# Moving three images' expert step from layer 0's front to a place beside layer 1's first convolution, in rounds of four 32-row parts

## The chip, the core and the metric

The kernel runs on one core of one Trainium2 chip. The metric is the device time of one execution in microseconds (us). The core has five engines with queues of their own: PE (matmul, with its weight loads shown apart as PEld), DVE (vector work), ACT (activations), POOL (GpSimd) and SP, which here only issues DMAs. The engines meet through semaphores. SBUF and PSUM are the memories on the core, HBM the one outside.

## The reference

Two residual layers on an fp32 tensor x of 4 images, 64 channels, 256 x 256 pixels. Layer 0 is x + L0(gn(x)), layer 1 the same with L1; gn is a group norm over 32 groups of two channels, whole image.

```python
# L0
h = gelu(conv3x3(x))                        # 64 -> 64
xa, k = split(conv1x1(h))                   # 64 -> 64 + 64
xs = gelu(vertical3(horizontal3(xa)))       # depthwise
gate = top2(softmax(mean_pixels(xs) @ gate_w.T))   # 3 experts per image
out = xs
for i in range(3):                          # ranks of 2, 4 and 8: 14 in all
    out = out + conv1x1(conv1x1(k, w2) * conv1x1(xs, w1), w3) * gate[:, i]
return conv1x1(out, proj)
# L1: weights rounded to 255 steps
h = relu(batchnorm(conv3x3(x)))
h = batchnorm(conv3x3(h))
return relu(h + x)
```

The batch norms run over all four images, so layer 1's second convolution starts only when the first is done for all images. The gate of an image needs the mean of xs over all its pixels.

## The kernel before, in words

An image is held as 128 partitions (64 channels times two row parities or two slots) by 128 pairs of rows. The units are: a group of 2 pairs (512 numbers per partition), an octet of 4 pairs, a chunk of 8 pairs (2048 numbers per partition, 1 MB). An image has 64 groups, 32 octets and 16 chunks.

The kernel has these stages. **Front** of layer 0, image by image: one step handles one octet, with the first convolution (`ps_c`, as a transform with products from the ring `v_ring` that POOL makes at line 413), the depthwise taps (`ps_a`), the projection of xs (`ps_p`), which is added into the chunk of x and written to HBM as `t1_d` (traffic group `t_d<-x`, line 587), and the experts' 14 ranks: `front_k` and `front_q` put k times xs, padded to 16 rows for each of 8 row groups, into the SBUF tile `low` (line 597), 512 numbers per partition for each of the 16 chunks. **Experts' step** ("out"): when an image's front has ended and its gate is known, `gate` scales the third expert matrices by the gate into `wm`, and `out_groups` makes y, the output of layer 0: a matmul of `low` with `wm` into `ps_o` (line 661), DVE adds it to the chunk of `t1_d` that `out_load` fetched (line 663), takes statistics for layer 1's group norm (line 666), and SP writes the chunk to `y_d` in four DMAs (line 671). `out_end` combines the statistics with two small matmuls (`ps_m`, `ps_v`). **First convolution** of layer 1 (`conv1`): for each chunk `conv1_load` fetches `y_d`, ACT applies the group norm (line 695) and makes the upper half of the fp32 split (line 700), DVE makes the lower half, y minus upper (`conv1_lower`, line 707), and PE runs 12 matmuls of 128 x 128 by 512 for each group (line 281); ACT moves the result out of PSUM (line 723), DVE takes statistics (line 728) and ACT's queue writes it to `h1_d`. **Second convolution**, and an **end stage** that adds and writes the output.

One step of `out_groups` works on two 64-row halves of `low` at once: half i of the partitions holds one octet, `wm` has 128 columns for one of two slots, and the two matmuls write two PSUM banks. It yields 1024 numbers per partition, half a chunk, so an image takes 32 such rounds.

The order of the work around the change is written out by hand. `at(step, order, call, ...)` enters a call in a plan; the plan is run through in the order of (step, order), and PE, SP, DVE and POOL take their instructions in exactly that order, each engine waiting only for its own data. ACT's order is the scheduler's. Front steps of image b are 32 b to 32 b + 31, and `CONV1` = 128 is the first step of the first convolution, whose steps are one group each: image b has the 65 steps from 128 + 65 b. The last front steps of image 3 are spread over the first ten of them (`tail`). Image b's out rounds stand in the front steps of image b + 1, one per step from 32 (b + 1) + 4; those of image 3 stand beside the first convolution, one in four steps from step 140:

```python
plan_out(b, CONV1 + 12 if last_one else (b + 1) * F_STEPS + 4, 0.25 if last_one else 1, 2)
```

PSUM is one pool of tiles of two banks: two tiles for "c", one for "a", one for "p"; "p" is shared by `ps_k`, `ps_q`, `ps_p`, `ps_o` and small matmuls. The first convolution uses only one bank of a tile: two tiles up to step 139, then three in turn. Chunks from HBM for the front and for the first convolution come into four buffers of the tag "in"; `out_load` has three buffers ("o"); the halves of a chunk have two buffers, so a chunk's halves can be written when PE has left the chunk two before it.

Of the kernel before, what the change touches and what calls it, by code (L numbers as in the profile page):

```python
# [12 lines left out]
ALU = mybir.AluOpType  # L13
# [5 lines left out]
P = 128  # L19

# [37 lines left out]
def conv_preact_kernel(ctx: ExitStack, tc: tile.TileContext, io, col128, colset, col64):  # L58
# [8 lines left out]
    psum = ctx.enter_context(tc.tile_pool(name="psum", bufs=1, space=PSUM))  # L67
# [4 lines left out]
    def bank(tag, name):  # L72

        return psum.tile([P, 2, GP, W], F32, tag=tag, name=name, bufs=BANKS[tag])

    def small(name):

        return bank("p", name)[:, 0, 0, :]
# [3 lines left out]
    t1_d = [dram.tile([P, NPAIR, W], F32, name=f"t1_d{b}") for b in range(B)]  # L82
    y_d = [dram.tile([P, NPAIR, W], F32, name=f"y_d{b}") for b in range(B)]
# [487 lines left out]
    def front_proj(b, n):  # L571

        ps = bank("p", f"ps_p_{b}_{n}")
        proj = c128("proj")

        rounds(
            *(
                [((ps[:, i], i ^ s, i, proj, xss[b, n][:, s].rearrange("p (a b) -> p a b", b=W), (0, GP)), dict(start=True, stop=True))]
                for i in range(2)
                for s in range(2)  # L580
            )
        )
        k, i = n // 2, 4 * (n % 2)
        t1 = xs_of[b, k][:, i : i + 4, 1 : 1 + W].rearrange("p (q s) w -> p s q w", s=2)
        nc.vector.tensor_tensor(t1, ps, t1, ALU.add)  # L585
        if n % 2 == 1:
            nc.sync.dma_start(t1_d[b][:, k * CPAIR : (k + 1) * CPAIR, :], xs_of[b, k][:, :, 1 : 1 + W])

    def front_q(b, j):
# [7 lines left out]
        nc.vector.scalar_tensor_tensor(low[:, j, :], ps, c128("e_b1"), k_sb.pop((b, j)), ALU.add, ALU.mult)  # L597


    wm, out_bias, ys, st_y = {}, {}, {}, {}  # L600

    def gate(b):
# [26 lines left out]
        for e, (i, j) in enumerate(((3, 4), (0, 5), (1, 2))):  # L629
# [4 lines left out]
        pick = stat.tile([P, 5, 3], F32, tag="pick", name=f"pick_{b}")  # L634
        of = c128("of").rearrange("p (i e) -> p i e", e=3)
        nc.vector.tensor_tensor(pick[:, 0:4, :], keep.unsqueeze(1).to_broadcast([P, 4, 3]), of, ALU.mult)
        nc.vector.tensor_tensor(pick[:, 4, :], keep, pb3, ALU.mult)
        row = stat.tile([P, 5], F32, tag="row", name=f"row_{b}")
        nc.vector.tensor_reduce(row, pick, AX.X, ALU.add)
        wm[b] = lstat.tile([P, 4, C], F32, tag="wm", name=f"wm_{b}")  # L640
        nc.vector.tensor_tensor(
            wm[b], row[:, 0:4].unsqueeze(2).to_broadcast([P, 4, C]), pw3.unsqueeze(1).to_broadcast([P, 4, C]), ALU.mult
        )
        out_bias[b] = stat.tile([P, 1], F32, tag="ob", name=f"ob_{b}")
        nc.vector.tensor_tensor(out_bias[b], row[:, 4:5], c128("proj_b"), ALU.add)
# [5 lines left out]
    def out_groups(b, j):  # L651


        if j == 0:
            st_y[b] = stat.tile([P, NG, 6], F32, tag="st_y", name=f"st_y{b}")
        k, slot = j // 2, j % 2
        ps = bank("p", f"ps_o_{b}_{j}")
        for i in range(2):
            rows = slice(i * C, i * C + C)
            w = wm[b][rows, 2 * slot : 2 * slot + 2, :]  # L660
            nc.tensor.matmul(flat(ps[:, i]), flat(w), low[rows, k, :], start=True, stop=True)  # L661
        y = ys[b, k].rearrange("p (i q s) w -> p s i q w", i=2, s=2)[:, slot]
        nc.vector.scalar_tensor_tensor(y, ps, out_bias[b], y, ALU.add, ALU.add)  # L663
        for i in range(2):
            g = 2 * j + i
            nc.vector.bn_stats(st_y[b][:, g, :], y[:, i])
            if g % CG == CG - 1:
                y = ys.pop((b, k))
                for half in range(2):
                    for slot in range(2):  # L670
                        nc.sync.dma_start(
                            y_v[b][half, slot ^ half][:, k * CG : (k + 1) * CG],
                            y[half * C : half * C + C, slot : CPAIR - 1 + slot : 2],
                        )
# [27 lines left out]
    def conv1_lower(b, k):  # L702
# [4 lines left out]
        nc.vector.tensor_tensor(lower, at_y, upper.bitcast(F32), ALU.subtract)  # L707

    def conv1(b, s):
# [5 lines left out]

        tag = "c" if b == 0 and s < 12 else "cca"[s % 3]
        ps = bank(tag, f"ps_h_{b}_{s}")[:, 0]
# [97 lines left out]
    def plan_out(b, t, per, order):  # L815

        for k in range(NCH):
            at(max(t + int((k - 1.5) * 2 / per) - 1, t - 2), 5, out_load, b, k)
        for j in range(NG // 2):
            at(t + int(j / per), order, out_groups, b, j)  # L820
        e = t + int(NG / 2 / per) + 1
        at_each(((e, 5.5), (e + 1, 5.5), (e + 1, 9.95), (e + 2, 5.5)), out_end(b))
# [10 lines left out]
    def plan_conv1(b):  # L833
        t = CONV1 + b * (NG + 1)
        if b == 0:
            at(t - 3, 0, lambda: halves.append(half_pads([half_tile(first_pool, f"half_10{j}", 2) for j in range(2)])))
            at(t, 12, conv1_open)
        for k in range(NCH):
# [11 lines left out]
    for b in range(B):  # L850
# [3 lines left out]
        last_one = b == B - 1  # L854
        plan_out(b, CONV1 + 12 if last_one else (b + 1) * F_STEPS + 4, 0.25 if last_one else 1, 2)
# [59 lines left out]
    for i, (b, k) in enumerate(chunks):  # L915
# [3 lines left out]
        for n in range(CG):  # L919
# [4 lines left out]
            ps = bank("cacp"[n], f"ps_h2_{b}_{k}_{n}")[:, 0]  # L924
# [63 lines left out]
def _layout(a):  # L988
# [44 lines left out]
    of = np.zeros((4, 2, 2, 2, 16, 3), f)  # L1033
    for i, (group, half) in enumerate(((0, 0), (1, 0), (1, 1), (0, 1))):
        of[i, :, group, half, np.arange(NLOW), expert] = 1.0
# [10 lines left out]
        "of": of.transpose(1, 2, 3, 4, 0, 5).reshape(P, 12),  # L1046
# [38 lines left out]
```

## Time and profile before

| what | value |
|---|---|
| median of 3 runs | 3538.37 us (3536.97 to 3542.3) |
| the profiled execution: its own time, its span | 3536.42 us, 3534.3 us |
| PE busy | 2942.4 us, 83% of the span |
| DVE, ACT, POOL busy | 2248.1, 1672.0, 631.2 us |
| share of the chain of waits that PE holds | 75% |
| DMA moved | 796.33 MB, mean 225 GB/s |
| stages, by their first and last matmuls in the timeline | front from 67 us, first convolution 1526 to 2342 us, second 2352 to 3078 us, end stage to 3534 us |
| out rounds: `ps_o` matmuls, additions (line 663), statistics (line 666) | 144.6, 163.7 and 164.7 us busy, 128 rounds |

The page gives busy times per engine, the span in 40 slices of 88 us, DMA traffic, the chain of work that ended last (followed back from the end, so that each piece is what the next waited for), the costliest groups, and DMA issues. An engine's idle time costs nothing where another engine is the bound; what matters is which wait ends last in the stage.

### The profile page before, as it was taken

What the parts mean: (1) busy time and instruction counts of PE and PEld (TensorE: products, weight loads), DVE (VectorE), ACT (ScalarE), POOL (GpSimd) and SP (SyncE); (2) the same over time, 40 slices, a digit from 0 to 9 for tenths busy, and PEclk for the clock granted to TensorE, in tenths of its full rate; (3) what the DMA queues carried; (4) which work ended last, traced back from release to release, by engine and by line L of the source; (5) the groups of instructions that cost most, each with busy time, mean ns of one, the idle gap of its engine ahead of it and who ended that gap; (6) DMA issues with size and microseconds to landing.
All of it is one profiled execution on the core that took longest, in us unless ns stands there. A gap on an engine that the chain in (4) does not pass through costs nothing.

```text
span 3534.3 us, 60792 instructions
## 1 busy us (share of the span) xinstructions
PE 2942.4 (83%) x25840; PEld 1941.7 (55%) x25840; DVE 2248.1 (64%) x2520; ACT 1672.0 (47%) x1706; POOL 631.2 (18%) x1250
## 2 busy tenths in 40 slices
PE   2999999999999999989999999989999999700000
PEld 1555555554555555547777788878888888600000
DVE  7666688878887777665666544444444444566666
ACT  0444434434433434446555566656666666422223
POOL 2444444433443444400000000000000000000000
PEclk9999999999999999999999999999999999955555
DMA  8564578667776666647776655545555553299999
GB/s 281 147 177 133 159 231 253 207 201 236 242 231 180 182 179 185 190 128 287 262 272 233 233 200 195 199 178 192 200 202 199 197 199 107 95 397 411 413 411 389
DMA packets 344031, 796.33 MB, mean 225 GB/s; under 512 B 19088, under 2 KB 281744, under 8 KB 282064
## 3 DMA queue, kind: packets, MB, share of 16 engines
q1 hardware_dynamic: 326912, 673.42, 56.8%
q10 hardware_dynamic: 16848, 119.02, 8.3%
q8 instruction: 203, 3.33, 0.4%
q14 instruction: 68, 0.56, 0.0%
HBM read 472.03 MB, written 320.34 MB: 224 GB/s over the span
## 4 chain that ended last, share of the span: by engine, by line
PE 75%; DMA 9%; DVE 6%; SPq 5%; ACT 3%; issue 1%; POOL 0%; DVEq 0%; ACTq 0%; POOLq 0%
PE ps_h L281 38%; PE ps_c L370 18%; PE ps_a L370 8%; DMA y_end<-y_d 5%; PE ps_o L661 3%; PE ps_k L561 3%; PE ps_p L370 3%; SPq L972 3%; DMA yn<-y_d 2%; SPq L967 2%; PE ps_q L594 1%; DMA xs_in<-in_x 1%; DVE h L964 1%; ACT v L963 1%; DVE st_x L317 1%
## 5 line engine op out<-in xcount | busy, mean ns | idle before, releaser
L281 PE MATMUL ps_h<-half,w_q 128*128 128x512 f32 x6168 | 1459.3, 397 | 14.6 <-DVE half L707 5.7
L281 PEld LDWEIGHTS ps_h<-half,w_q 128*128 128x128 f32 x6168 | 1162.8, 189 | 324.2 <-ACT h L723 15.6
L413 POOL TENSOR_TENSOR v_ring<-x 128x256 f32<-128x256 f32 x1024 | 596.7, 615 | 159.7 <-PE ps_c L370 109.1
L728 DVE BATCH_NORM_STATS2 st_h<-h 128x6 f32<-128x512 f32 x252 | 173.4, 691 | 356.5 <-ACT h L723 356.3
L370 PE MATMUL ps_c<-v_ring,u 64*64 64x256 f32 (+1 forms) x6472 | 389.0, 371 | 10.2 <-POOL v_ring L413 5.5
L370 PE MATMUL ps_c<-v_ring,c1s 64*64 64x256 f32 (+1 forms) x6472 | 386.6, 368 | 0.5 <-DVE ps_c L481 0.5
L370 PEld LDWEIGHTS ps_c<-v_ring,u 64*64 64x64 f32 x6472 | 254.2, 133 | 238.6 <-issue 79.2
L370 PE MATMUL ps_a<-h,av 64*64 64x512 f32 (+1 forms) x3568 | 381.8, 530 | 2.6 <-DVE t L540 2.6
L370 PEld LDWEIGHTS ps_c<-v_ring,c1s 64*64 64x64 f32 x6472 | 262.0, 133 | 134.5 <-issue 39.2
L928 DVE BATCH_NORM_STATS2 st_h<-h 128x6 f32<-128x512 f32 x256 | 174.0, 690 | 239.5 <-ACT h L927 239.5
L479 ACT ACTIVATE m<-ps_c 128x512 f32<-128x512 f32 x128 | 76.6, 598 | 473.5 <-PE ps_c L370 466.5
L723 ACT ACTIVATE h<-ps_h,m,scale_w 128x512 f32<-128x512 f32 x256 | 196.1, 770 | 206.4 <-PE ps_h L281 202.4
L554 ACT ACTIVATE xs<-t 128x1024 f32<-128x1024 f32 x128 | 135.4, 1058 | 322.1 <-DVE t L543 295.6
L927 ACT ACTIVATE h<-ps_h,m,scale_w 128x512 f32<-128x512 f32 x256 | 197.3, 771 | 182.2 <-PE ps_h L281 181.9
L963 ACT ACTIVATE v<-y_end,shift,gn 128x2048 f32<-128x2048 f32 x64 | 133.8, 2092 | 311.1 <-DMA y_end<-y_d 304.3
L295 DVE TENSOR_TENSOR half<-h,half 128x2304 fp32r<-128x2304 f32 (+1 forms) x65 | 163.8, 2521 | 147.6 <-ACT half L293 147.6
L964 DVE SCALAR_TENSOR_TENSOR h<-h,ss,v 128x2048 f32<-128x2048 f32 x64 | 150.2, 2350 | 150.2 <-ACT v L963 149.7
L585 DVE TENSOR_TENSOR x<-ps_p,x 128x1024 f32<-128x1024 f32 x128 | 156.4, 1222 | 131.4 <-PE ps_p L370 99.0
L370 PEld LDWEIGHTS ps_a<-h,av 64*64 64x64 f32 x3568 | 163.7, 133 | 114.4 <-issue 79.7
L537 DVE SCALAR_TENSOR_TENSOR t<-ps_a,m,t 128x1020 f32<-128x1020 f32 x128 | 163.6, 1278 | 83.7 <-ACT t L536 83.7
L487 ACT ACTIVATE h<-ps_c,c1b 128x512 f32<-128x512 f32 x256 | 176.1, 748 | 36.4 <-PE ps_c L370 36.4
L663 DVE SCALAR_TENSOR_TENSOR y<-ps_o,ob,y 128x1024 f32<-128x1024 f32 x128 | 163.7, 1279 | 18.5 <-PE ps_o L661 15.3
(159 smaller groups left out, 2645.2 us busy)
## 6 DMA issues: line engine op xcount, KB each, us to landing
h_d<-h ACTq DMA_DIRECT2D x113, 1024.0 KB, 4.1
h<-h_d SPq DMA_DIRECT2D x64, 1152.0 KB, 5.1
yn<-y_d SPq DMA_DIRECT2D x60, 1152.0 KB, 8.3
xs_in<-in_x SPq DMA_DIRECT2D x64, 1024.0 KB, 7.7
x<-in_x SPq DMA_DIRECT2D x256, 256.0 KB, 4.9
t_d<-x SPq DMA_DIRECT2D x64, 1024.0 KB, 5.3
y<-t_d SPq DMA_DIRECT2D x64, 1024.0 KB, 7.9
y_d<-y SPq DMA_DIRECT2D x256, 256.0 KB, 5.1
```

Source lines behind the costliest of these rows:

```text
L281: nc.tensor.matmul(ps[:, 0:n, :], w[:, kx, m, :], t[:, i + m : i + m + n, kx : kx + W], start=(j == 0), stop=(j == len(terms) - 1),)
L295: nc.vector.tensor_tensor(lower, y[:, a:e, :], upper.bitcast(F32), ALU.subtract)
L370: last[:] = [nc.tensor.matmul(ps[o, at_out[0] : at_out[1], :], w[i], rhs[i], **flags)]
L413: nc.gpsimd.tensor_tensor(v_ring[:, o : o + 2, p, :], *terms[p])
L487: nc.scalar.activation(h.rearrange("p q (c e) -> p e q c", e=2), c[:, t].rearrange("p (e q c) -> p e q c", e=2, q=GP), AF.Gelu, bias=c1_bi ...
L663: nc.vector.scalar_tensor_tensor(y, ps, out_bias[b], y, ALU.add, ALU.add)
L723: nc.scalar.activation(h, ps, AF.Identity, bias=c128("b1"), scale=w_scale["w1"])
L728: nc.vector.bn_stats(st[:, s, :], h)
L927: nc.scalar.activation(o, ps, AF.Identity, bias=c128("b2"), scale=w_scale["w2"])
L928: nc.vector.bn_stats(st[:, k * CG + n, :], o)
L963: nc.scalar.activation(v, y, AF.Identity, bias=shift[:, b : b + 1], scale=gn2[b][:, 1:2])
L964: nc.vector.scalar_tensor_tensor(h, h, ss2[:, 0:1], v, ALU.mult, ALU.add)
```

## The change

- Images 1 to 3 do their out rounds beside the first convolution: image 1 in steps 142 to 182 (during image 0's convolution), image 2 in 191 to 246, image 3 in 256 to 311, 16 rounds each. Image 0 keeps its 32 rounds in image 1's front.
- A round of images 1 to 3 is a whole chunk: four matmuls, each of a 32-row part of the ranks with a 128-column `wm`, into four PSUM banks (`ps_o`, one buffer). `wm` and its selector `of` have two row layouts in place of four slots. DVE works on the four banks one at a time: an addition and a statistics instruction of 512 numbers each. Image 0's rounds have two 32-row parts.
- `front_q` of images 1 to 3 writes each chunk of ranks to HBM (`low_d`), and `low_load` reads it back beside `out_load`, into the two buffers of tag "k".
- `front_proj` writes a chunk of `t1_d` in three DMAs in place of one, with the lower 64 partitions' two slots exchanged.
- `conv1_lower` runs on GpSimd in place of DVE.
- At step 140 the PSUM pool is closed and a new one opened: four one-bank tiles for both convolutions and the small matmuls, and one of four banks for `ps_o`.

```diff
+    def banks_open():
+        banks0.close()
+        psum.append(ctx.enter_context(tc.tile_pool(name="psum1", bufs=1, space=PSUM, reuse_waits="tile")))
...
         if n % 2 == 1:
-            nc.sync.dma_start(t1_d[b][:, k * CPAIR : (k + 1) * CPAIR, :], xs_of[b, k][:, :, 1 : 1 + W])
+            x = xs_of[b, k][:, :, 1 : 1 + W]
+            t1 = t1_d[b][:, k * CPAIR : (k + 1) * CPAIR, :]
+            nc.sync.dma_start(t1[0:C], x[0:C])
+            for slot in range(2):
+                nc.sync.dma_start(t1[C:P, 1 - slot :: 2], x[C:P, slot::2])
...
+        if b > 0:
+            nc.sync.dma_start(low_d[b][:, j, :], low[:, j, :])
...
+    def low_load(b, k):
+        lows[b, k] = work.tile([P, GF], F32, tag="k", name=f"low_{b}_{k}")
+        nc.sync.dma_start(lows[b, k], low_d[b][:, k, :])
+
+    def out_octets(b, k, octets):
...
+        if b == 0:
+            ranks = low[:, k, :]
+            ps = bank("p", f"ps_o_{b}_{k}_{octets[0]}")
+        else:
+            ranks = lows.pop((b, k))
+            ps = psum[1].tile([P, 4, GP, W], F32, tag="o", name=f"ps_o_{b}_{k}", bufs=1)
+        for n, i in enumerate(octets):
+            for g in range(2):
+                rows = slice(64 * i + 32 * g, 64 * i + 32 * g + 32)
+                nc.tensor.matmul(flat(ps[:, 2 * n + g]), flat(wm[b][rows]), ranks[rows], start=True, stop=True)
+        for n, i in enumerate(octets):
+            for g in range(2):
+                y = ys[b, k][:, 4 * i + g : 4 * i + g + 3 : 2, :]
+                nc.vector.scalar_tensor_tensor(y, ps[:, 2 * n + g], out_bias[b], y, ALU.add, ALU.add)
+                nc.vector.bn_stats(st_y[b][:, 4 * k + 2 * i + g, :], y)
+        if 1 in octets:
+            y = ys.pop((b, k))
+            for half in range(2):
+                for g in range(2):
+                    nc.sync.dma_start(
+                        y_v[b][half, g][:, k * CG : (k + 1) * CG],
+                        y[half * C : half * C + C, g::2],
+                    )
...
-        nc.vector.tensor_tensor(lower, at_y, upper.bitcast(F32), ALU.subtract)
+        nc.gpsimd.tensor_tensor(lower, at_y, upper.bitcast(F32), ALU.subtract)
...
-        tag = "c" if b == 0 and s < 12 else "cca"[s % 3]
-        ps = bank(tag, f"ps_h_{b}_{s}")[:, 0]
+        ps = bank("c", f"ps_h_{b}_{s}")[:, 0] if len(psum) == 1 else bank1(f"ps_h_{b}_{s}")
...
+    def plan_out(b, t, e):
+
+        steps = [t + (e - 6 - t) * k // (NCH - 1) for k in range(NCH)]
+        for k in range(NCH):
+            for call in (out_load, low_load):
+                at(steps[k - 2] if k > 1 else t - 1, 0.2, call, b, k)
+            at(steps[k], 2, out_octets, b, k, (0, 1))
+        at_each(((e - 5, 15), (e - 4, 15), (e - 3, 15), (e - 2, 15)), out_end(b))
...
+            at(t + 12, -1, banks_open)
...
-        last_one = b == B - 1
-        plan_out(b, CONV1 + 12 if last_one else (b + 1) * F_STEPS + 4, 0.25 if last_one else 1, 2)
+        if b == 0:
+            plan_out0(F_STEPS + 4)
+        else:
+            step = CONV1 + (b - 1) * (NG + 1)
+            plan_out(b, step + (14 if b == 1 else -2), step + NG - 5)
```

## The prediction, made before the changed kernel was run

> **What bounds the kernel now.** I read the page's slices first, then the chain of waits in the three stages concerned, then the stretches (busy time of each engine in a window), then the groups by shape.
>
> ```profile
> PE   2999999999999999989999999989999999700000
> DVE  7666688878887777665666544444444444566666
> DMA  8564578667776666647776655545555553299999
> ```
>
> PE is at nine tenths from 88 us to 3000 us, in the front and in both convolutions alike. So moving PE work from one stage to the other gains nothing by itself; the change pays only if the step gets cheaper on PE. DMA is the row to watch: it has room in the first convolution now, and most of the step's traffic is being moved there.
>
> The price of a round in the front can be read by comparing two octets without one (image 0, chain of waits) with two that have one (image 3, timeline of PE):
>
> ```profile
> 194.69 3.62 PE ps_c L370 x64
> 204.47 3.62 PE ps_c L370 x64
> 215.24 3.62 PE ps_c L370 x64
> ```
>
> ```profile
> 1260.58 1.96 PE L370 MATMUL ps_c<-v_ring,u 64*64 64x256 f32 x32
> 1262.47 1.13 PE L661 MATMUL ps_o<-low,wm 64*128 64x512 f32 x4
> ...
> 1272.44 1.96 PE L370 MATMUL ps_c<-v_ring,u 64*64 64x256 f32 x32
> ...
> 1283.43 1.94 PE L370 MATMUL ps_c<-v_ring,u 64*64 64x256 f32 x29
> ```
>
> Two steps take 215.24 - 194.69 = 20.55 us without rounds and 1283.43 - 1260.58 = 22.85 us with two, so a round costs 1.15 us: its matmuls, and nothing that hides. Beside the first convolution the chain shows
>
> ```profile
> 1613.75 1.06 PE ps_o L661 x4
> 1614.81 11.41 PE ps_h L281 x48
> 1626.22 1.06 PE ps_o L661 x4
> 1627.28 11.41 PE ps_h L281 x48
> ```
>
> Four groups and a round take 12.47 us. Later, without rounds, the chain has 768 matmuls (64 groups) in 179.87 us: 2.81 a group, 11.24 for four. A round costs 1.23 us there. The clock is at 1.00 in both places.
>
> DMA, by stretches (length; PE, PEld, DVE, ACT, POOL busy; clock; DMA share; GB/s):
>
> ```profile
> 1790.00:1797.00 7.00, 7.00 (x32) 5.64 (x31) 3.88 (x4) 4.35 (x4) 0.00 (x0) 1.00 0.90 197
> 1797.00:1805.00 8.00, 8.00 (x35) 5.68 (x34) 4.15 (x6) 3.16 (x3) 0.00 (x0) 1.00 0.98 401
> 1650.00:1800.00 150.00, 150.00 (x629) 110.81 (x628) 92.39 (x99) 87.18 (x73) 0.56 (x2) 1.00 0.75 263
> ```
>
> With image 3's rounds at a quarter of the later rate, this stage already holds the DMA engines for 0.75 of the time at 263 GB/s, or 263/0.75 = 351 GB/s while they work. With loads of several kinds queued they reach 401; right after y's writes, 197.
>
> **The change part by part**, against the profiled execution (3536.4 us, its span 3534.3), which is 2 us under the median.
>
> *Front.* Images 1 and 2 lose 64 rounds there: 64 x 1.15 = 73.6 us saved. Sixty lie in full steps, four where image 3's last octets mix with the first groups of the convolution. In those four the timeline shows PE waiting 1.46, 0.96 and 1.43 us more on DVE or ACT around `ps_o`, which goes too: another 4 (0 to 8). DVE's part of a round (1.28 + 2 x 0.69) lies beside PE in the front and saves nothing.
>
> *Four parts at once.* 48 rounds of a whole chunk stand where 32 half-chunk rounds of image 3 stood. The trace has no four 32-row parts. Nearest are the four column parts of `ps_k` and `ps_q` (0.96 and 1.08 us for four, from 123.1/128 and 69.1/64) and the two row parts of `ps_o`: a part more costs nothing in either. I take 1.23: 48 x 1.23 - 32 x 1.23 = +19.7. From below 5 less; from above, if only two of the four ran together, 48 x 1.06 = 51 more. The Trainium skill ("TensorE: Matmul & The Clock Gate", Part 3, measured speedup) speaks a little against the change: it states 3.07 times for four 32-row parts, not 4. An estimate by that rule makes a round 1.06 x 4/3.07 = 1.38 us and the sum 15 us dearer; no run here shows it yet.
>
> *DVE.* These groups carry it:
>
> ```profile
> L666 DVE BATCH_NORM_STATS2 st_y<-y 128x6 f32<-128x512 f32 x256 | 164.7, 685 | 4.4
> L707 DVE TENSOR_TENSOR half<-yn,half 128x2304 fp32r<-128x2304 f32 x60 | 152.6, 2543 | 2.6 <-ACT half L700 2.6
> L597 DVE SCALAR_TENSOR_TENSOR low<-ps_q,m,k 128x512 f32<-128x512 f32 x64 | 48.0, 750 | 38.0 <-PE ps_q L594 38.0
> ```
>
> A 512-wide addition out of PSUM takes 0.75 us (line 597 has that shape), so a round is 4 x 0.75 + 4 x 0.69 = 5.8 us of DVE. Image 1's rounds come every 40/15 = 2.67 steps, 2.67 x 2.81 + 1.23 = 8.7 us; with 2.67 statistics of the convolution (1.8) DVE has 7.6 us of work in 8.7. It fits only because the lower halves leave it (2.54 per four steps). For images 2 and 3 a round comes every 3.67 steps, 11.5 us. Cost 0. Queued behind an addition that waits for its chunk are the convolution's statistics, and behind those ACT's next output buffer: if y comes late, that is how it reaches PE. Image 0's rounds cost DVE 0.2 us more, under PE.
>
> *Lower halves on GpSimd.* Line 413's 128x256 subtraction takes 615 ns on POOL, so 2304 columns take 9 x 0.615 = 5.5 us. In steady state a half starts when ACT's copy (2.13) ends, and PE needs it a chunk (11.2 us or more) after that copy could start: over 3 us spare, 0. Where PE waited directly behind it (1598.35 to 1600.97, first chunks) it costs 3 us (0 to 9, as three such halves are on the chain). The rule in "GPSIMD Engine Reference" (4.1, engine selection), which sends two-input elementwise work to VectorE, makes it 4497/2048 x 2304 = 5.1 us as an estimate; the term would be 2.5.
>
> *SP and buffers.* SP gets two more `t_d` issues in all 64 chunks and 48 writes and 48 loads of ranks, 0.3 to 0.6 us each, in queues that wait for data anyway; in the front it loses as many y issues. 0; without that cover, some 1 us a chunk. New waits: `low_load` stands on SP until PE has done the round two before, which y's writes of that round outlast; `ps_o` has one buffer, so PE's next round waits for four additions (about 5.1 us of 8.7). Both 0 while DVE keeps up. One-bank PSUM tiles give the convolution four buffers in place of two or three: 0, at best the 6 us or so of the 15.6 that PE waited for ACT in both convolutions.
>
> *Two more `out_end`* beside the convolution. Image 3's is there already:
>
> ```profile
> 2010.63 0.59 PE L262 MATMUL ps_v_y<-d_y,m 128*128 128x1 f32 x2 [6.38 <-DVE d_y L259]
> ```
>
> It sits behind statistics, which sit behind an ACT that waited 4.76 us for a chunk of y. In the front each cost some 1.5. I take +4 each, 8 - 3 = +5 (-3 to +11).
>
> *Transfers.* Image 1's rounds: ten chunks of the convolution (1.18 in, 1.05 out) and 16 of y (1.05 in, 1.05 out, 0.26 ranks), less 3.7 fetched ahead: 56.4 MB. PE's time there is 40 x 2.81 + 16 x 1.23 = 132 us, so it asks 427 GB/s: more than either rate. At 401 it takes 141 us (+9), at 351 161 (+29). Images 2 and 3: 64.7 MB in 55 x 2.81 + 16 x 1.23 = 174 us, 372 GB/s: 0 at 401, +10 each at 351. A full queue is the nearest row, but SP will leave gaps; I take +17, +4 and +4 = +25 (9 to 49).
>
> Sum: -73.6 - 4 + 19.7 + 3 + 5 + 25 = -24.9 us. From 3536.4 that is 3511.5, and 3513.5 against the median.
>
> **The rivals.** (a) *The transfers hide.* If they run at 401 with what was fetched ahead, and the two `out_end` are free, the sum is -24.9 - 16 - 8 = -49: about 3489. For it: the stretch at 401 with PE at 8.00 of 8. Against: every load of the convolution now stands on SP behind y's writes, which wait for DVE.
>
> (b) *The transfers become the bound, slower than before.* SP issues in order: y's four writes wait for the additions, the next chunk's load waits for an older chunk's writes to land, and convolution loads stand behind both, so the engines idle and then work in the 197 GB/s manner. The three stages move 56.4 + 2 x 64.7 = 185.8 MB in 480 us. The gain is used up when they take 50 us longer, 185.8/530 = 350 GB/s mean: just the rate at which they now work when they work. At 320 they take 580 us, +101 in place of +25, so -24.9 + 76 = +51: 3589.
>
> (c) *Four parts run two by two*: 3513.5 + 51 = 3564. Against it, columns of `ps_k`.
>
> (d) *The front doesn't shorten*, because POOL, SP or the added writes take the rounds' place: 3513.5 + 73.6 = 3587. Image 0's front, at 20.55 us for two steps with the same work, speaks against.
>
> **How the numbers follow.** Forecast 0.50, with its own range 3494 to 3535; (a) 0.19, (b) 0.22, (c) 0.06, (d) 0.03. A measurement can tell about 0.2%, 7 us, from no change. Faster by more: 0.87 of the forecast and all of (a), 0.62. Within: 0.13 of the forecast and a fifth of (b), 0.11. Slower: 0.27. The low end, 3472, takes all good bounds (-24.9 - 16 - 8 - 5 - 4 - 3 - 6 = -67); the high end, 3578, leaves out the far half of (b) and (d).
>
> **What would show it.** Right: two front steps of images 2 and 3 in about 20.6 us; `ps_o` rounds of 1.06 to 1.1 us with eight instructions; over 350 GB/s in image 1's rounds; GpSimd rows of about 5.5 us with no PE wait on them after the first chunks; PE waits of some 20 us in image 1's rounds, released by DMA, ACT or DVE. Wrong: a first convolution that grows by more than the front shrinks, SP rows with long waits at y's writes while DMA is under 0.9; a round of 2 us; or front steps still at 22.8.

## The result, and the profile after

The change makes the kernel slower. Its median is 3618.36 us (3616.68 to 3623.19, four runs) against 3539.14 us before on the same chip: a ratio of 1.0225, 95% interval 1.0208 to 1.0243. The forecast was 3513.5 us and its range ended at 3578. The profiled execution has a span of 3616.6 us, 82.3 above that of before.

The table gives the stages of single profiled executions, in us. A front reaches from the first transform instruction of an image on DVE to that of the next image (image 3's to its own last one); "conv1 0" to "conv1 3" are the first convolution's images, by the ends of ACT's moves out of PSUM, and "between" is the stretch from DVE's last transform instruction of image 3's front to the end of the convolution's step 11, from where "conv1 0" is counted. The second convolution (729 to 731) and the end stage (462 to 465) did not move, with one exception that is named under E17. "Conv1" is the sum of its four images. E1 to E18 are the experiments of the next section.

| kernel | front 0 | 1 | 2 | 3 | between | conv1 0 | 1 | 2 | 3 | conv1 | span |
|---|---|---|---|---|---|---|---|---|---|---|---|
| before | 330.1 | 370.8 | 376.7 | 360.9 | 84.4 | 169.7 | 203.2 | 193.0 | 178.9 | 744.8 | 3534.3 |
| after | 336.3 | 395.6 | 366.5 | 330.8 | 72.8 | 233.7 | 217.8 | 214.9 | 180.7 | 847.1 | 3616.6 |
| E1 statistics' load first | 326.0 | 372.6 | 345.2 | 330.6 | 72.9 | 226.9 | 223.4 | 215.7 | 180.6 | 846.6 | 3562.5 |
| E9 without 50 MB of writes | 329.2 | 371.5 | 345.2 | 332.4 | 71.2 | 201.1 | 206.5 | 205.3 | 178.2 | 791.1 | 3506.1 |
| E10 y in one long write | 329.5 | 372.6 | 343.7 | 331.2 | 72.5 | 218.9 | 206.0 | 204.6 | 181.3 | 810.8 | 3530.0 |
| E11 four long writes | 329.5 | 372.2 | 345.2 | 330.6 | 72.6 | 224.6 | 215.7 | 209.2 | 180.6 | 830.1 | 3549.9 |
| E12 two images, spread | 329.3 | 371.8 | 379.2 | 333.9 | 77.4 | 188.9 | 209.4 | 209.4 | 182.3 | 790.0 | 3548.0 |
| E13 the same, early loads | 329.0 | 371.5 | 378.6 | 334.2 | 77.6 | 181.3 | 198.2 | 197.7 | 180.6 | 757.8 | 3515.6 |
| E14 the change's own steps | 329.5 | 372.6 | 378.9 | 333.8 | 77.5 | 163.9 | 218.5 | 217.3 | 180.1 | 779.8 | 3540.0 |
| E18 long pieces | 329.3 | 372.3 | 381.9 | 333.7 | 74.6 | 171.8 | 202.7 | 192.1 | 179.8 | 746.4 | 3504.4 |

So the loss has two places. The fronts and the stretch behind them gave 9.3 + 11.6 = 20.9 us where 77.6 were forecast. The convolution grew by 102.3 us where 52.7 were forecast. That is 56.7 and 49.6 us beyond the forecast. The two together, 102.3 - 20.9 = 81.4, are the loss.

The slices of the page show where PE lost its nine tenths, and that the DMA row is at eight and nine tenths beside the rounds:

```profile
PE   2999999998999999878899999989999999800000
DMA  8565578766664454379899998545555553299999
```

**The front.** An event from image 1's front. First SP's timeline (start, length, line, traffic): three writes of `t1_d`, the write of the ranks, and only then the loads of the next image's chunk for the statistics.

```profile
547.32 0.89 SPq L601 DMA_DIRECT2D t_d<-x  x1
548.25 2.59 SPq L603 DMA_DIRECT2D t_d<-x  x2
550.94 0.76 SPq L615 DMA_DIRECT2D low_d<-low  x1
551.74 5.74 SPq L322 DMA_DIRECT2D xs_in<-in_x  x2
```

DVE's timeline then shows a statistics instruction before which DVE sat idle for 4.18 us until that load had landed (idle time and its releaser in brackets):

```profile
555.85 1.27 DVE L329 BATCH_NORM_STATS2 st_x<-xs_in 128x6 f32<-128x512 f32 x2
561.30 0.69 DVE L329 BATCH_NORM_STATS2 st_x<-xs_in 128x6 f32<-128x512 f32 x1 [4.18 <-DMA xs_in<-in_x]
```

Behind it on DVE stands the addition of line 597, which empties the bank "p", and for that bank PE waits. The first row is the same work in an undisturbed step:

```profile
536.59 1.92 PE L573 MATMUL ps_k<-h,wk 128*32 128x512 f32 x16
...
563.17 3.64 PE L573 MATMUL ps_k<-h,wk 128*32 128x512 f32 x16 [3.67 <-DVE x L597]
```

The wait costs twice: these matmuls take 3.64 us here and 1.92 in the undisturbed step, and the granted clock is 0.50 from 563 to 567 us. From 480 to 1120 us DVE waited for the statistics' loads 33.5 us in all, 7 times, 5.9 us at the longest:

```profile
DVE st_x L329 <- DMA xs_in<-in_x: 33.5, 7, 5.9
```

In the same window the kernel before has no such wait, and E1, the experiment that issues these loads earlier, has 0.5 us of it.

Where the front is not held up, in image 3's, the chain of waits has the forecast length; two steps take 1312.06 - 1291.56 = 20.5 us:

```profile
1291.56 3.62 PE ps_c L382 x64
...
1302.28 3.62 PE ps_c L382 x64
...
1312.06 3.62 PE ps_c L382 x64
```

**The convolution.** The stretches from the first to the last round of images 1, 2 and 3 (length; PE, PEld, DVE, ACT, POOL busy; clock; DMA share; GB/s):

```profile
1594.00:1767.00 173.00, 140.92 (x589) 98.38 (x588) 107.42 (x160) 69.98 (x58) 46.55 (x10) 0.90 0.89 307
1804.00:1990.00 186.00, 178.67 (x800) 131.96 (x799) 117.89 (x179) 99.90 (x84) 64.97 (x15) 0.99 0.97 343
2022.00:2207.00 185.00, 176.78 (x791) 130.39 (x790) 117.89 (x178) 98.48 (x83) 62.35 (x14) 0.99 0.98 344
```

In the rounds of images 2 and 3 the DMA engines are full (0.97 and 0.98) at 343 and 344 GB/s, with DVE and POOL far from full. In those of image 1 they reach 0.89, and the chain of waits shows a round hand over from transfer to transfer: y's writes (line 697) land, which frees the buffer for the load of y, behind which the ranks are loaded, for which PE waits:

```profile
1671.61 1.55 SPq L697
1673.20 6.23 DMA y_d<-y
1679.57 0.33 SPq L667
1680.00 7.66 DMA low<-low_d
...
1687.79 1.91 PE ps_o L687 x8
```

That reading suggested that an order on SP could mend it. The experiments say otherwise.

### The profile page after: what moved, and what is told of

Same layout as the page of the kernel before. It is cut to its first block, busy times and chain, and to the rows that moved or that the text cites. A ratio compares the mean times of both kernels' runs of the same rounds, so it can differ in the third digit from the quotient of the medians.

```text
span 3616.6 us, 61538 instructions
## 1 busy us (share of the span) xinstructions
PE 2928.0 (81%) x25840; PEld 1956.2 (54%) x25840; DVE 2120.2 (59%) x2584; ACT 1664.6 (46%) x1702; POOL 927.7 (26%) x1314
## 4 chain that ended last, share of the span: by engine, by line
PE 69%; DMA 12%; DVE 7%; SPq 6%; ACT 2%; issue 2%; POOL 1%; ACTq 0%; DVEq 0%; POOLq 0%
PE ps_h L293 34%; PE ps_c L382 17%; PE ps_a L382 8%; DMA y_end<-y_d 5%; PE ps_k L573 3%; PE ps_p L382 3%; SPq L1009 3%; DMA yn<-y_d 2%; DMA xs_in<-in_x 2%; PE ps_o L687 2%; SPq L1004 2%; PE ps_q L610 2%; DMA low<-low_d 1%; DVE st_x L329 1%; DVE h L1001 1%
## 5 line engine op out<-in xcount | busy, mean ns | idle before, releaser
L293 PE MATMUL ps_h<-half,w_q 128*128 128x512 f32 x6168 | 1477.5, 400 | 30.5 <-POOL half L733 16.9
L733 POOL TENSOR_TENSOR half<-yn,half 128x2304 fp32r<-128x2304 f32 (+1 forms) x64 | 297.0, 4640 | 582.8 <-ACT half L726 580.7
L382 PEld LDWEIGHTS ps_c<-v_ring,c1s 64*64 64x64 f32 x6472 | 270.3, 134 | 95.9 <-issue 15.8
L721 ACT ACTIVATE yn<-yn,gn 128x2304 f32<-128x2304 f32 (+1 forms) x64 | 146.9, 2296 | 172.7 <-DMA yn<-y_d 168.7
```

The lines of the kernel that those rows point to most:

```text
L293: nc.tensor.matmul(ps[:, 0:n, :], w[:, kx, m, :], t[:, i + m : i + m + n, kx : kx + W], start=(j == 0), stop=(j == len(terms) - 1),)
L382: last[:] = [nc.tensor.matmul(ps[o, at_out[0] : at_out[1], :], w[i], rhs[i], **flags)]
L733: nc.gpsimd.tensor_tensor(lower, at_y, upper.bitcast(F32), ALU.subtract)
```

## The experiments

Theories: the **order theory** for the front (loads late behind writes on SP); for the convolution the **loop theory** (SP's order makes each round wait for a landing), the **rate theory** (the DMA engines can't carry more), the **GpSimd theory** (the slower halves), and later the **landing theory** (loads issued too late for the time that they take). Each difference in the table of stages is between single executions. Seven kernels with the same convolution traffic (the change, E1 to E3, E5, E6, E8) have a sum of 835.6 to 847.1, and three with that of E13 (E13, E15, E16) one of 757.8 to 769.9. So a difference of up to 12 us between two sums can be chance, and where it matters the medians are given beside it. Of the kernels, E2, E4, E9, E10 and E11 compute other values than the reference.

**E1, the statistics' load first.**

```diff
-at(t + int((k - 1) * CG / per), 11.5, stats_load, b, k, "s", 2)
+at(t + int((k - 1) * CG / per), 5.5, stats_load, b, k, "s", 2)
```

> The changed kernel with one order changed: in the front, the load of the next image's statistics chunk is issued by SP ahead of the step's three t_d writes and the write of ranks, not behind them. Nothing else is moved; the bytes are the same. Order theory (the front lost its gain because the statistics' loads stand on SP and in the queue behind writes that wait for DVE, and DVE in order waits for them): the fronts of images 1 and 2 (395.6 and 366.5 us in the changed kernel) lose 15 to 30 us each, total 3560 to 3590 us; the first convolution stays. Rate theory (the stage asks for more bytes than the DMA engines carry, whatever the order): no stage moves by more than 5 us, total 3612 to 3624. GpSimd theory (the slower lower halves cost the time): no change either, since the fronts have none.

Measured: 3563.22 us, 1.0067 of before (1.0044 to 1.009), 55 us less than the change. Fronts 1 and 2 lost 23.0 and 21.3 us, the convolution stayed at 846.6. The order theory holds for the front: one order on SP was worth nearly all of its missing gain. E2, E3 and E4 ran beside it, without this edit; E5, E6 and E8 to E16 and E18 contain it.

**E2, one write of t1_d.**

```diff
-nc.sync.dma_start(t1[0:C], x[0:C])
-for slot in range(2):
-    nc.sync.dma_start(t1[C:P, 1 - slot :: 2], x[C:P, slot::2])
+nc.sync.dma_start(t1, x)
```

> The changed kernel with each chunk of t1_d written in one DMA as before, not in three; the two slots of the lower 64 partitions are then not exchanged, so y has two slots swapped there: same work, other values. The ranks are still written to HBM. Order theory: two SP issues of 0.6 to 1 us fewer for each of 64 chunks, so statistics' loads and the y loads behind them are earlier: front of images 0 to 3 together 15 to 40 us shorter, total 3577 to 3602. If only the write of ranks holds SP (it waits for DVE's line that makes them), under 8 us. Rate theory: bytes are the same, 0 to -5. GpSimd theory: 0.

Measured: 3571.29 us; the four fronts take 1392.1 us together in place of 1429.2. Two issues fewer a chunk give 37 of E1's 55. The total is 6 us under the range that the order theory gave.

**E3, ranks first**, and **E4, no ranks through HBM.**

```diff
-for call in (out_load, low_load):
+for call in (low_load, out_load):
```

> The changed kernel with the load of a chunk of ranks issued ahead of the load of the same chunk of y on SP, not behind it. Order theory: PE waited 25.7 us for ranks beside image 0's convolution because their 0.26 MB stand behind a 1 MB load that itself waits on SP for a buffer; these waits go, but the addition still needs the same load of y: image 0's convolution (233.7 us) loses 5 to 25 us, total 3590 to 3612. Rate theory: the engines are full in that stage, the wait only changes its name from ranks to y: 0 to -5, total 3612 to 3624. GpSimd theory: 0.

```diff
-nc.sync.dma_start(low_d[b][:, j, :], low[:, j, :])
...
-ranks = lows.pop((b, k))
+ranks = low[:, k, :]
...
-for call in (out_load, low_load):
+for call in (out_load,):
```

> The changed kernel without the ranks' way through HBM: no write of ranks, no load; the rounds of images 1 and 2 use whatever ranks are in the tile then (values differ, work on PE and DVE is the same). It takes away 48 writes and 48 loads of 0.26 MB. Order theory: the write of ranks no longer holds SP in the front and PE no longer waits for ranks: fronts of images 1 to 3 (395.6, 366.5, 330.8) lose 20 to 50 us together, the first convolution 20 to 50, total 3520 to 3575. Rate theory: the convolution stages lose only what 12.6 MB take at 350 GB/s, 36 us over 48 rounds and less where they are hidden: 10 to 36, the fronts 0 to 10, total 3570 to 3605. GpSimd theory: 0 to -10.

Measured: 3615.76 and 3616.9 us, both as the change. E3's sum for the convolution is 840.9, E4's 853.9. PE's waits for ranks in the rounds (1580 to 2210 us) fell from 25.7 us to 17.2 in E3 and to none in E4, without a gain, so they were only the last of several waits. E4 fits neither theory: it moves 12.6 MB less beside the convolution, and ACT's waits for the convolution's own loads of y rose from 95.1 to 128.5 us (1850 to 2200 us) while DMA's share there fell from 0.95 or more to 0.89 to 0.93. Why is open.

**E5, loads behind the writes on SP.**

```diff
-at(steps[k - 2] if k > 1 else t - 1, 0.2, call, b, k)
+at(steps[k - 2] if k > 1 else t - 1, 2.5 if k > 1 else 0.2, call, b, k)
```

> The kernel with the statistics' load first, and one more order changed: beside the first convolution the loads of y's chunk and of its ranks for the round two later are issued by SP behind the round's own four writes of y, not ahead of them (the first two chunks excepted). Same bytes, same buffers. Loop theory (y's load stands on SP until the writes of the round before have landed, the ranks' load until PE has done this round, and this round's writes and the convolution's loads stand behind both, so that a round costs one landing and all issues in series): image 0's convolution falls from 226.9 us to 185-205, images 1 and 2 from 223.4 and 215.7 to 200-212; total 3500 to 3535. Rate theory (the 16 DMA engines are full, order can't help): conv1 of images 0 to 2 stays within 8 us in sum; total 3553 to 3572.

Measured: 3564.31 us, the convolution 843.2. The loop theory, as an order on SP, falls.

**E6, lower halves on DVE.**

```diff
-nc.gpsimd.tensor_tensor(lower, at_y, upper.bitcast(F32), ALU.subtract)
+nc.vector.tensor_tensor(lower, at_y, upper.bitcast(F32), ALU.subtract)
```

> The kernel with the statistics' load first and the lower halves on DVE again (2.54 us each there, 4.64 us on GpSimd in the changed kernel's profile). GpSimd theory (PE's waits in the first convolution come from the slower halves): the first convolution (846.6 us for four images) loses 15 to 40 us, total 3522 to 3550. Loop and rate theories: PE's direct waits for halves (some 17 us in three stages) go, but DVE gets 2.54 us more for each chunk, 9.3 us of work for 8.7 us of PE in image 1's rounds, so y's additions come later: conv1 -10 to +25, total 3552 to 3590.

Measured: 3572.05 us, the convolution 846.9 against 846.6 (7.4 of the 9 us by which it is behind E1 lie in the stretch before it). The GpSimd theory falls for the full change. **E7, that part alone in the kernel before:**

> The kernel before with one part of the change alone: the lower halves of the first convolution on GpSimd. By the prediction's term +3 us (0 to 9). If the slower half costs wherever PE waits right behind it (at each stage's first chunks and at each late load), +6 to +15; if DVE's relief counts, -5 to 0.

Measured: 3556.31 us, 1.005 of before (1.0033 to 1.0067): 17 us dearer, 15.9 of it in the convolution, and there in images 0, 2 and 3. So, as far as E6 and E7 show, it costs something where DMA is not the bound, and nothing where it is. ACT's waits for loads of y rose with it from 51.2 to 103.3 us (1500 to 2350 us). SP issues such a load when a half has released its buffer, so a later half may make a later load; no run tests this.

**E8, the convolution's loads four steps earlier**, with the change's rounds.

```diff
-load, ready = t + 4 * k - 9, t + 4 * k - 4
+load, ready = t + 4 * k - 13, t + 4 * k - 4
```

> The kernel with the statistics' load first, and the first convolution's own loads of y issued four steps earlier (nine steps of 2.81 us ahead of ACT, not five); no buffer is added. Landing theory (with y's and the ranks' transfers beside it such a load lands 8 to 14 us after its issue, and five steps are 14 us, so ACT and then PE wait for it): images 1 and 2 of the convolution go from 223.4 and 215.7 us to 203-212, image 0's (whose round asks for 427 GB/s) from 226.9 to 215-226; total 3530 to 3552. Rate theory (bytes alone): the wait moves to other transfers, the three stages stay within 8 us in sum, total 3553 to 3572.

Measured: 3561.02 us, 2 us under E1, and the convolution 842.3. Alone it does nothing that can be told from chance.

**E9, 50 MB less on ACT's queue.**

```diff
-if s % CG == CG - 1:
+if s % CG == CG - 1 and b == B - 1:
     nc.scalar.dma_start(h1_d[b][:, k * CPAIR : (k + 1) * CPAIR, :], h_out.pop(b))
...
-nc.sync.dma_start(h, h1_d[b][:, k * CPAIR : (k + 1) * CPAIR + 1, :])
+nc.sync.dma_start(h, h1_d[B - 1][:, k * CPAIR : (k + 1) * CPAIR + 1, :])
```

> The kernel with the statistics' load first and without the writes of the first convolution's result of images 0 to 2 to HBM (ACT's queue issues them); the second convolution reads image 3's result four times instead, in the same amounts. It takes 50 MB of DMA away from the three stages and nothing from SP's queue. Rate theory: image 0's convolution asks for 46 MB in 132 us beside image 1's rounds, 348 GB/s, and images 1 and 2 ask for 48 MB in 174 us, 275 GB/s: nearly all of the loss goes, the first convolution falls from 846.6 us to 760-785, total 3475 to 3502. Loop theory (SP's order and the landing of y's writes set the round): the landings get somewhat shorter, the order stays: 846.6 to 805-835, total 3520 to 3552.

Measured: 3512.37 us, the convolution 791.1, 55.5 less. That lies between the two ranges, nearer to the rate theory's 760 to 785 than to 805. Nothing on SP was changed beside the rounds. In the stretches of images 2 and 3, the second and third below, PE is busy for every microsecond:

```profile
1540.00:1684.00 144.00, 135.69 (x592) 96.00 (x593) 106.84 (x161) 69.33 (x58) 41.96 (x9) 0.95 0.89 299
1718.00:1889.00 171.00, 171.00 (x775) 126.34 (x775) 118.44 (x178) 97.10 (x82) 60.79 (x13) 1.00 0.90 289
1924.00:2095.00 171.00, 171.00 (x775) 126.38 (x775) 118.47 (x178) 96.38 (x82) 60.78 (x13) 1.00 0.90 288
```

Its chain of waits prices the round of four parts undisturbed. The round and four groups take 1.07 + 11.40 = 12.47 us, just what the half-chunk round and four groups took before:

```profile
1931.39 11.40 PE ps_h L293 x48
1942.79 1.07 PE ps_o L687 x8
```

**E10, y's chunk in one long write** (images 1 to 3). Is it the bytes, or their form?

```diff
-for half in range(2):
-    for g in range(2):
-        nc.sync.dma_start(y_v[b][half, g][:, k * CG : (k + 1) * CG], y[half * C : half * C + C, g::2])
+nc.sync.dma_start(y_d[b][:, k * CPAIR : (k + 1) * CPAIR, :], y)
```

> The full change with the statistics' load first, and y's chunk of images 1 to 3 written in one DMA of long pieces, not in four of 1 KB pieces (the rows then stand in another order: same bytes, other values). If the four issues on SP or the short pieces set the round, the first convolution falls from 846.6 us to 800-835, total 3515 to 3550. If the sum of bytes sets it, within 10 us: 3552 to 3572.

Measured: 3533.32 us, 0.9976 of before (0.9967 to 0.9985), the convolution 810.8: 35.8 us less for the same bytes. SP's timelines of one round, E1 and then E10, show one side of it:

```profile
2008.59 3.73 SPq L697 DMA_DIRECT2D y_d<-y  x4
2012.42 1.40 SPq L714 DMA_DIRECT2D yn<-y_d  x1
```

```profile
2007.11 0.32 SPq L703 DMA_DIRECT2D y_d<-y  x1
2007.52 0.39 SPq L717 DMA_DIRECT2D yn<-y_d  x1
```

The four writes hold SP for 3.73 us, and the convolution's load behind them is issued that much later in the round. The stretches of E10's images 1 and 2 show the other: 26 and 25 GB/s more than in the change (16 and 29 more than in E1) at no higher share.

```profile
1545.00:1706.00 161.00, 139.27 (x591) 97.90 (x590) 105.99 (x160) 69.32 (x58) 44.55 (x10) 0.92 0.89 333
1739.00:1912.00 173.00, 172.24 (x782) 127.09 (x779) 119.91 (x179) 97.69 (x82) 63.74 (x15) 1.00 0.96 368
```

**E11, four writes of 4 KB pieces** (images 1 to 3), to part the two. Here `at_d` is `k * CPAIR + g * CG`.

```diff
-nc.sync.dma_start(y_v[b][half, g][:, k * CG : (k + 1) * CG], y[half * C : half * C + C, g::2])
+nc.sync.dma_start(y_d[b][half * C : half * C + C, at_d : at_d + CG, :], y[half * C : half * C + C, g * CG : g * CG + CG])
```

> The full change with the statistics' load first, and y's chunk of images 1 to 3 written in four DMAs as in the change, but of 4 KB pieces in place of 1 KB pieces (the rows then stand in another order: same bytes, same number of issues, other values). With one DMA of long pieces the first convolution took 810.8 us in place of 846.6. If the short pieces hold the DMA engines, nearly the same gain: 804-822. If the three further issues on SP did it, none: 840-850. Half and half would be 822-838.

Measured: 3544.99 us, the convolution 830.1. By the sums of stages, the pieces carry 16.5 of the 35.8 us, and the step from four issues to one, which also makes the pieces 8 KB long, the other 19.3. By the ratios to the kernel before (1.0067, 1.0011, 0.9976) it is 20 and 12 us, so the split is a rough one. The packets in the traces bear it out. Their medians are 46 ns for 1 KB (E1), 159 for 4 KB (E11) and 309 for 8 KB (E10), and a chunk of y is 1024, 256 or 128 of them on 16 engines. An estimate from these gives 2.94, 2.54 and 2.47 us of all engines a chunk. Over 48 chunks that is 19 us for the longer pieces of E11 and 3 for the still longer ones of E10, which by this estimate leaves most of the last step to the issues on SP. So the rate theory holds in a wider form: what counts is not bytes alone, but the time that their pieces take, and beside it that of their issues.

**E12, only images 2 and 3 beside the convolution, evenly spread**, **E13, the same with early loads**, and **E14, the same two images at the change's own steps.**

```diff
-plan_out(b, step + (14 if b == 1 else -2), step + NG - 5)
+plan_out(b, *((CONV1 + 14, CONV1 + 97), (CONV1 + 101, CONV1 + 183))[b - 2])   # E12, E13, or:
+plan_out(b, *((CONV1 + NG - 1, CONV1 + 2 * NG - 10), (CONV1 + 2 * NG, CONV1 + 3 * NG - 9))[b - 2])   # E14
```

> A version meant to beat both kernels: the statistics' load first; image 1's expert step back in image 2's front (32 rounds of two parts); only images 2 and 3 beside the first convolution, their 32 rounds spread evenly, one in 5.5 steps over steps 142 to 311; image 3's ranks read from the tile where they still are, only image 2's go through HBM; loads behind the round's writes on SP. By both theories: the front of image 2 gets back 33 to 37 us (to about 380), the first convolution falls from 846.6 to 745-765 us, since a round now comes with 16.6 us of PE time and asks for 5.2 MB, some 315 GB/s. Total 3485 to 3515. If the rate alone is the bound, at most 10 us of DMA waits are left; if the loop alone is, under 5.

> The spread version (image 1 in the front, images 2 and 3 spread over steps 142 to 311) with the convolution's loads of y issued four steps earlier. Landing theory: its first convolution, 790 us, falls to 748-762, since the rounds ask for some 315 GB/s, under what the engines have carried; total 3505 to 3525. Rate theory: the waits come back elsewhere, total 3538 to 3556.

> The spread version with early loads, but images 2 and 3 at the change's own steps (191 to 246 and 256 to 311: a round in 3.67 steps, asking for 350 to 376 GB/s) and none beside image 0's convolution. Rate theory: image 0's convolution takes 152-160 us, images 1 and 2 come back to 208-222 each (198 in the spread version), so the sum of the three, 577 us there, is 570 to 600, total 3508 to 3540. If in the full change only image 1's rounds (427 GB/s) hurt, and their backlog carried over into the later stages: images 1 and 2 at 196-202, the sum 545-562, total 3484 to 3502.

Measured: 3550.92, 3527.53 and 3539.8 us; against before 1.0031, 0.9961 (0.9943 to 0.9978) and 0.9999. E12 missed its range: at 278 to 314 GB/s there were still waits, ACT's above all, for loads of y. They land 7.7 to 17.2 us after their issue (1600 to 2100 us) and are planned five steps (14 us) ahead. E13 mends that with the edit that gave nothing in E8: the convolution falls by 32.2 us in the profiled executions, though E13's is the fastest of its five and 10 us under their median, and by the medians the gain is 23 us. So the landing theory holds for the spread version. That the edit needs a rate below the full one is the reading that fits E8 and E13; the two kernels differ in more than that. E14 has no rounds beside image 0, and yet images 1 and 2 are at 218.5 and 217.3, as in the change; the three images take 599.7 us where E13, with the same rounds at a slower pace, takes 577.2. So those images lose by their own pace, not by a backlog of image 1's rounds.

**E15, E13's lower halves on DVE**, **E16, those of the first four chunks only.**

> The same as the spread version with early loads, with the lower halves on DVE. If GpSimd's 4.64 us stand on the path once the loads are early, 8 to 20 us faster than that version; if they are hidden, within 4 us; if DVE, in order, makes the halves late behind additions that wait for y, up to 10 us slower.

> The spread version with early loads, and the lower halves of image 0's first four chunks on DVE, the rest on GpSimd: in the first 12 steps PE waits right behind each half, and there are no rounds yet. If those halves stand on the path, 4 to 9 us less than the spread version with early loads (profiled at 3515.6 us, median 3527.5): profile 3506 to 3512; if the loads of y set these steps, within 3 us.

Measured: 3531.27 and 3527.77 us, against E13's 3527.53: no difference that these runs can tell. Their convolutions took 769.9 and 760.2 us where E13's took 757.8.

**E17, three writes of t1_d in the kernel before.**

> The kernel before with one part of the change alone: each chunk of t1_d is written in three DMAs, not one (without the exchange of slots). Order theory for the front: two more issues ahead of the statistics' load on SP are enough to make it late, since taking two of the three away gave 45 us: fronts of images 0 to 2 (330.1, 370.8, 376.7 us) grow by 8 to 20 us each, total 3555 to 3590. If it takes the write of ranks as well (it waits on SP for DVE), under 8 us in sum, total 3536 to 3547.

Measured: 3581.99 us, 1.0131 of before (1.0109 to 1.0153): 40 us dearer, by the three writes alone. The pieces are no shorter: the traces of both kernels have 262,656 packets of 1 KB and, but for two, equally many of 8 and 9 KB, so what is left is the issues and their order. Its profiled execution (3602.94) has an end stage 22 us longer than any other and is read for the fronts only: 9.1, 7.1, 9.8 and 5.1 us longer.

**E18, long pieces in a version that computes the whole reference.** E13, with the even rows of a chunk ahead of the odd ones in HBM, so that y's writes have 4 KB pieces and are two:

```diff
-y_v = [t.rearrange("(par c) (q half) w -> half par c q w", par=2, half=2) for t in y_d]
+y_v = [t.rearrange("(par c) (k half q) w -> half k c par (q w)", par=2, half=2, q=CG) for t in y_d]
...
-y = ys[b, k][:, 4 * i + g : 4 * i + g + 3 : 2, :]
+y = ys[b, k][:, g * CG + 2 * i : g * CG + 2 * i + 2, :]
...
+y = y.rearrange("p (g q) w -> p g (q w)", g=2)
 for half in range(2):
-    for g in range(2):
-        nc.sync.dma_start(y_v[b][half, g][:, k * CG : (k + 1) * CG], y[half * C : half * C + C, g::2])
+    nc.sync.dma_start(y_v[b][half, k], y[half * C : half * C + C])
```

> The spread version with early loads, and y kept in HBM with the even rows of a chunk ahead of the odd ones, so that its writes have 4 KB pieces (two DMAs a chunk) for every image; t1_d is written in four DMAs of an order that lets DVE fill y's chunk so, ACT and GpSimd make the halves of a chunk in three instructions, and the end stage takes the rows in two parts. If pieces hold the engines: the first convolution 757.8 us falls to 742-754, total 3505 to 3524. If the further small instructions of ACT and GpSimd stand on the path: 3525 to 3545.

Measured: 3507.93 us, 0.9902 of before (0.9886 to 0.9919): 35 us faster than the kernel before and 110 faster than the change, and 20 under E13. It has longer pieces and also two issues a chunk in place of four; the two were not parted here. PE loses 0.56 us in 496 beside the rounds:

```profile
1585.00:1836.00 251.00, 250.44 (x1113) 189.74 (x1113) 138.56 (x206) 147.32 (x163) 101.02 (x62) 1.00 0.92 316
1854.00:2099.00 245.00, 245.00 (x1092) 185.97 (x1092) 137.95 (x206) 147.67 (x163) 98.58 (x61) 1.00 0.92 312
```

## Why the prediction was wrong, by its own steps

- **"SP and buffers": the step that failed first.** It put the added issues at 0, "in queues that wait for data anyway". E1 and E17 show 55 and 40 us. (E17 has the issues of `t_d` alone, without the writes of ranks.) The cover did not exist in the front: behind those issues stood a load for which DVE, in order, waited, and behind DVE stood PE's bank. The text asked who is queued behind an addition on DVE, but not who is queued behind `t_d`'s writes on SP. Its own price without the cover, 1 us for each of 64 chunks, comes near in size, but by luck: it counted the time of the issues, and the cost is PE's waits behind a late load, with the halved clock after some of them.
- **"Front", -73.6 and -4:** right in size. The two steps of 20.5 us, and with E1's order the fronts and the stretch between give 64.1 + 11.5 = 75.6. The order itself doesn't make this gain: the fronts of images 0 and 1, whose rounds stay where they were, take 330.1 and 370.8 us before and 326.0 and 372.6 in E1.
- **"Four parts at once", +19.7:** right; 1.07 us for a round and 12.47 with four groups: eight instructions in four parts take what four in two parts took. Rival (c) is out. The 1.38 us that the prediction estimated from 3.07 times ("TensorE: Matmul & The Clock Gate", Part 3, measured speedup) were not seen; what one part alone takes, and so the speedup itself, no run here shows.
- **"Transfers", +25 (9 to 49): mis-sized.** From the first to the last round PE's work is 40 x 2.81 + 15 x 1.23 = 130.9 us for image 1 and 173.0 for images 2 and 3 each; measured are 173.0, 185.6 and 184.6, so +66. The lower row it used was right: 307/0.89 = 345, 344/0.98 = 351 GB/s while they work. It then took a middle between that and 401, a rate seen for 8 us; 351 throughout is its upper end, 49. For images 2 and 3 that end is what came (12 us each for its 10); the other 13 us lie in image 1's rounds, 42 for its 29. E10 and E11 show a good part of why 401 did not carry over: y's short pieces and four issues, which before came once in eight steps, now come once in 2.67 or 3.67, and are worth 36 us (30 by the medians). The rest of the convolution's growth, 102.3 - 19.7 - 66 = 17 us where 8 were forecast, was not taken apart.
- **"Lower halves on GpSimd", +3:** no cost in the full change (E6), 17 us in the kernel before (E7). One takes 4.64 us, less than the 5.5 that were worked out. It is also less than the 5.1 us estimated from the figure in "GPSIMD Engine Reference" (4497 ns for 2048 columns, in its section 3.1). So the duration was put too high, and in the kernel before the price was put too low all the same.
- **"DVE", 0:** holds as to its work; 107.4 us of 173 in image 1's rounds. **"Two more `out_end`"**, +5: not separated.
- **The rivals.** (a) is out. (b) has come in its number: 53.1 + 63.8 + 63.6 MB in 544 us are 332 GB/s, below its point of 350. By its formula 185.8/332 is 560 us, 55 more than the sum had. Its reason has not come: it saw engines that idle behind SP's order, but in the rounds of images 2 and 3 they are at 0.97 and 0.98, and E5's other order on SP gained no more than chance would. Only in image 1's rounds, at 0.89, may it have a part. (d) has come for 56.7 of the 77.6 us, through SP. What was set against it, two steps in 20.55 us in image 0's front, came from a kernel with one write of `t_d` a chunk and none of ranks, so it could not speak to the added writes. With both, -24.9 + 55 + 55 = +85, measured +82. The two were weighed as cases that exclude each other, with 0.22 and 0.03; but both come from the step's added writes and loads, and the range that took each alone ended below their sum.

## What to carry to other kernels

When a step is moved or its writes are split, list for every queue what stands behind each new issue, and follow it to the engine that waits in order; an issue on an idle-looking SP is free only if nothing behind it is needed soon. Price a transfer-heavy stage at the rate that the engines show while they are busy with such pieces, and count pieces and issues as well as bytes. Earlier loads did not help where the engines were full (2 us by the medians at 340 GB/s, E8) and did in a slower-paced version (23 us at 313, E13).

## What the runs showed of the hardware that was not expected

- For the same bytes, 4 KB in place of 1 KB pieces in y's writes alone were worth 16.5 us in 48 rounds (E11; 20 by the ratios). "DMA: Bandwidth & Descriptors" (its table of key figures) sets the length for line rate at 512 B; the 1 KB pieces here are above it and still cost time.
- The same page ("Where 436 GB/s comes from") gives about 358 GB/s as what binds between HBM and SBUF, one core's half of its HBM stack. The change's 343 and 344 at a full share looked like that limit. In this program on one core, E10's 368 in a stretch of 173 us and some 412 in the end stage of the change are above it.
- An idle time of 3.67 us on PE was followed by a granted clock of 0.50, and 16 matmuls took 3.64 in place of 1.92 us. "TensorE: Matmul & The Clock Gate" (Part 1) says the same of an idle window of some 3.4 us.
- Four writes of y held SP for 3.73 us in a round of E1, one of the same bytes for 0.32 in a round of E10.
